# Mixture-of-experts stage: fewer buffers for the returning rows of the first image, and other places for their sums and transposes

## The chip, the cores and the metric

The kernel runs on one core of a Trainium2 chip. The metric is the device time of one execution in microseconds (us). The core's engines work side by side: TensorE (PE) multiplies matrices and transposes, VectorE (DVE) and ScalarE (ACT) work on elements, GpSimd (POOL) does so too and issues gathers, and SyncE (SP) issues plain transfers. Each engine takes its instructions in the order in which the program was laid out, so an instruction that waits holds up all that stand behind it on its engine. Transfers (DMAs) run on 16 DMA engines that all queues share.

## The reference

Four layers are applied in turn to x of shape (2, 128, 56, 56), each as x = x + layer(group_norm(x)): an attention, a 3x3 convolution, a mixture of experts on 2x2 patches, and a pair of Mamba scans. The change lies in the third layer, where its result is handed to the fourth:

```python
xp = patches(group_norm(x))                # 1568 tokens of 512 numbers, 784 of each image
probs = softmax(xp @ router_w)             # 8 experts
topv, topi = top_k(probs, 2); topv = topv / topv.sum()
for e in range(8):
    val, g = split(xp @ w1[e], 2)          # w1[e]: 512 x 2048
    out += gate[:, e:e+1] * ((val * sigmoid(g)) @ w2[e])    # w2[e]: 1024 x 512
x = x + unpatch(out)
```

The fourth layer begins with the group norm of this x, image by image.

## The kernel before, in words

**Routing.** Every token goes to two experts. The tokens are sorted by image and expert into tiles of 128 slots (`SLOTS`); `route` works out which expert serves each tile, which token fills each slot, and in which two slots each token's results will lie (`self.slots`). Two numbers are known when the program is laid out: the first 25 tiles (`fewest`) always exist, and the tiles 0 to 19 (`ahead` is 20) are sure to hold all that belongs to the first image. How many tiles there are beyond 25 is read at run time (`tc.Switch`); with these inputs there are 28.

**One tile** (`run`, lines 1323 to 1448). A gather of token rows (`xr`, an indirect DMA on POOL's queue, four buffers), four transposes on PE (`xr_ps`, L1369) and a copy on DVE (`xs_c`, L1371). Then `up`: 128 PE instructions with the first weight matrix (`h_ps`, L1380), in four parts of 32: for each half c of the hidden numbers first the gate's part and then the value's. ACT takes the sigmoid of the gate (`sg`, L1392), DVE multiplies (`ht`, L1394). Then `down`: 16 PE instructions with the second matrix (`o_ps`, L1400); ACT scales by the token's share (`ot`, L1403) and stores the tile to `os` in DRAM from its own queue (L1404). `down` of tile j-1 stands behind `up` of tile j.

**Weights.** SP loads the first matrix of a tile (4096 KB, L1341) and the second (2048 KB, L1347), each into one of two buffers. The second matrix's load waits for the `down` that used its buffer last, and the first matrix's load of the next tile stands behind it in SP's queue.

**The way back for the first image** (`combine`, lines 1450 to 1497, as a generator driven by `arrive`). The image has seven blocks of 112 tokens. For each block, `fetched` issues two gathers from `os` on POOL's queue (L1314, tiles `g0` and `g1`, 112 rows of 2 KB each), one for each of the token's two experts. DVE adds the two (L1486), PE transposes the sum in four pieces (`y_ps`, L1489), and one turn later DVE adds these to x (L1462) and takes the statistics (L88). After the last block come three turns for the group norm (L100, L104, L116). `LEAD` tells how many blocks are gathered before the first sum; `gathered` gives each table `LEAD + 1` buffers. A gather can reuse its buffers when the block that held them has been transposed.

**The order of the work.** One `next(beside)` is one turn of that generator. `turns` tells for each of the tiles 20 to 24 (keys 0 to 4) at which of five spots turns are taken: 0 to 3 are the ends of the four parts of `up`, 4 is the end of `down` of the tile before. In `spot`, `issue_after(traced[0])` places what the turn issues on PE behind the last PE instruction traced, and `issue_after(shaped[0])` does the same on DVE. POOL gets no such tie. Within these bounds a planner lays out each engine's order, by the program's order and by what it holds ready. What is left over of the generator runs before the Switch.

Of the kernel before, what the change touches and what calls it, by code (L numbers as in the profile page):

```python
# [1013 lines left out]
class PatchExperts:  # L1014
# [308 lines left out]
    def run(self, wpool, work, ps, beside):  # L1323
# [25 lines left out]

        traced, shaped = [None], [None]  # L1350

        turns = {0: (4, 4), 1: (1, 3), 2: (0, 1, 4), 3: (0, 1, 2, 3, 4), 4: (0, 0, 1, 2)}

        def spot(j, at):
            if j < self.fewest:
# [149 lines left out]

MAMBA_STATES, MAMBA_RANK, MAMBA_TAPS = 16, 8, 4

LEAD, LEAD2 = 5, 3

POOLED = {"f": (0, 1, 2, 8, 9), "b": (0, 1, 10, 11)}  # L1510

# [139 lines left out]
def mamba_pair(net, out, wts, combine, keep, norms):  # L1651
# [19 lines left out]
    with ExitStack() as ctx:  # L1671
# [425 lines left out]
        with tc.manual_schedule(engines={E.PE, E.Activation, E.DVE, E.Pool, E.SP}):  # L2097
            second = arrive_by_scalar(net, combine, 1, gathered, wide_bank, mm, keep, norms, LEAD2)
            first = min(agenda)
            for step in range(first, 0):  # L2100
                run(step)
                for _ in range((LEAD2, 0, 0, 0, 0, 0, 1, 0, 1, 0, 1, 1, 3, 1)[step - first] if step - first < 14 else 0):
                    next(second, None)
                fetch(step + 1)
        with tc.manual_schedule(engines={E.PE, E.Activation, E.DVE, E.Pool, E.SP}):
# [5 lines left out]
            for n, (h, u) in enumerate(units):  # L2111
                if n + 1 < len(units):
                    who, i = units[n + 1]
                    who.decay(i)
                fetch(n)
                if u % 2 == 0 and not (h.by_pool(u) and h.by_pool(u + 1)):
                    h.read_out(u)
                if u % 2 == 0 and n + 6 < len(units):
                    who, i = units[n + 6]
                    who.send_c(i // 2)  # L2120
                if n + 4 < len(units):
                    who, i = units[n + 4]
                    who.push(i)
                h.scan(u)
                if done:
                    done.pop().close()
                waiting.append((h, u))
                if n in (9, 13):
                    place["tag"] = "mm"
                    next(second)  # L2130

                quota = 0 if u == 3 and n > 3 else 2 if u == 7 and n > 7 else 1
                for _ in range(quota):
                    if len(waiting) > 3:
                        who, i = waiting.pop(0)
                        who.collect(i)
                        if i == UNITS - 1:
                            done.append(who)
                run(n)
# [4 lines left out]
            for step in range(len(units), max(agenda) + 1):  # L2144
                run(step)
                fetch(step + 1)
# [111 lines left out]
```

## Time and profile before

| what | value |
|---|---|
| median of 3 runs | 3005.71 us (3002.7 to 3007.07) |
| the profiled execution's own time | 3010.8 us |
| its span in the trace | 3009.1 us |
| PE busy | 2688.4 us (89% of the span) |
| DVE busy | 2180.9 us (72%) |
| ACT busy | 1854.5 us (62%) |
| POOL busy | 1446.6 us (48%) |
| DMA moved | 369.30 MB |
| tiles of experts on PE, first to last | about 1030 to 1656 us |
| gathers of the first image, first and last issue | 1493.0 and 1515.7 us |
| its transposes, first and last | 1514.8 and 1559.4 us |

The trace gives each instruction's start and duration from the span's start, and in brackets how long its engine was idle before it and whose end released it. A view of stretches gives, for each stretch of time, the busy time of each engine, the granted share of the TensorE clock (PEclk) and the share of time in which the DMA engines were busy. "DMA to landing" is the time from the issue of a transfer to the arrival of its last bytes.

### The profile page before, as it was taken

To read this page: it belongs to the slowest core of one execution; us is meant where nothing else is said; L and a number is where in the kernel's file an instruction comes from. 1 tells how busy PE (TensorE), PEld (TensorE's weight loads), DVE (VectorE), ACT (ScalarE), POOL (GpSimd) and SP (SyncE) were. 2 spreads that over 40 slices of the span, in tenths; PEclk is the share of its full clock that TensorE was granted. 3 is DMA by queue.
4 is the path that set the end of the run, shared out by engine and by line. 5 is a ranking of instruction groups with operands and counts; after the bars stand their busy time and mean duration, and the time that the engine had idled before them with its cause. 6 is when DMAs were issued, how large, how long until landed. Compare 5 with 4: busy or idle time off the path is not lost. (4 is left out here: it accounts for less than half of the span.)

```text
span 3009.1 us, 39362 instructions
## 1 busy us (share of the span) xinstructions
PE 2688.4 (89%) x14926; PEld 1273.6 (42%) x14926; DVE 2180.9 (72%) x1849; ACT 1854.5 (62%) x2951; POOL 1446.6 (48%) x792
## 2 busy tenths in 40 slices
PE   7999999999999799999999788888888888888874
PEld 3333333333325687878777323333333333233321
DVE  5978999999886400010020589999999999999996
ACT  5778778887761100000011588888888888988884
POOL 3000010001232100000110689999999999999995
PEclk9999999999989799999999889999999889999987
DMA  1000000000002587878885644555555465544460
GB/s 56 1 1 1 1 1 1 1 1 1 1 1 61 208 317 296 328 301 321 321 305 211 146 117 114 122 136 139 119 121 117 117 142 128 129 115 121 117 145 26
DMA packets 158222, 369.30 MB, mean 123 GB/s; under 512 B 25190, under 2 KB 115398, under 8 KB 154422
## 3 DMA queue, kind: packets, MB, share of 16 engines
q1 hardware_dynamic: 135778, 339.30, 37.6%
q0 software_dynamic: 5136, 14.70, 1.6%
q10 hardware_dynamic: 17092, 12.53, 1.3%
q8 instruction: 122, 2.00, 0.3%
q14 instruction: 94, 0.77, 0.1%
HBM read 297.89 MB, written 17.20 MB: 105 GB/s over the span
## 5 line engine op out<-in xcount | busy, mean ns | idle before, releaser
L1940 POOL TENSOR_TENSOR dBu<-dtu,Bs 128x896 f32<-128x896 f32 x448 | 922.0, 2093 | 22.3 <-DMA Cs<-far 6.6
L1959 DVE TENSOR_TENSOR_SCAN h<-dA,dBu 128x896 f32<-128x896 f32 x448 | 882.2, 2008 | 34.1 <-ACT dA L1929 29.5
L620 ACT ACTIVATE ex<-sc 128x896 f32<-128x896 f32 (+1 forms) x700 | 602.7, 917 | 129.2 <-PE sc L617 117.7
L1981 PE MATMUL y<-h,both 128*64 128x448 f32 x1792 | 464.1, 609 | 82.8 <-POOL h L1968 75.7
L627 DVE TENSOR_TENSOR ex_sum<-ex_sum,ex 128x1792 f32<-128x1792 f32 (+1 forms) x238 | 492.5, 2069 | 37.8 <-ACT ex L620 23.8
L1380 PEld LDWEIGHTS h_ps<-xs_c,w 128*128 128x128 f32 x3584 | 407.7, 194 | 27.3 <-ACT ot L1403 15.4
L1380 PE MATMUL h_ps<-xs_c,w 128*128 128x128 f32 x3584 | 412.5, 278 | 7.2 <-DMA w<-in_L_conv_w_dram 5.8
L617 PE MATMUL sc<-q,k 32*128 32x448 f32 (+1 forms) x2800 | 405.6, 590 | 3.3 <-ACT ex L620 2.7
L1970 DVE TENSOR_TENSOR h<-h,c_ps 128x1792 f32<-128x1792 f32 (+1 forms) x168 | 326.5, 1944 | 28.8 <-ACT c_ps L1947 11.3
L635 PE MATMUL av<-ex,va 128*32 128x448 f32 (+1 forms) x2800 | 337.0, 556 | 0.1
L1394 DVE TENSOR_TENSOR ht<-h_ps,sg 128x512 f32<-128x512 f32 x56 | 38.5, 691 | 395.7 <-PE h_ps L1380 338.8
L582 POOL TENSOR_TENSOR a_e<-a_e,a_inv 112x784 f32<-112x784 f32 x14 | 41.6, 2974 | 586.3 <-ACT ex L620 394.5
L1929 ACT ACTIVATE dA<-dt,f_A 128x448 f32<-128x448 f32 x448 | 282.7, 635 | 51.1 <-DVE h L1959 43.4
L1929 ACT ACTIVATE dA<-dt,b_A 128x448 f32<-128x448 f32 x448 | 282.9, 635 | 32.7 <-DVE h L1959 23.8
L1981 PEld LDWEIGHTS y<-h,both 128*64 128x64 f32 x1792 | 117.9, 146 | 352.5 <-issue 209.9
L1314 POOL DMA_INDIRECT xr<-xd,whom x28 | 28.1, 1004 | 487.0 <-PE xr_ps L1369 445.9
L1968 POOL TENSOR_TENSOR h<-h,Cs 128x1792 f32<-128x1792 f32 (+1 forms) x70 | 252.7, 3610 | 11.2 <-PE conv_ps L1802 4.3
L617 PEld LDWEIGHTS sc<-q,k 32*128 32x128 f32 (+1 forms) x2800 | 138.3, 182 | 232.0 <-issue 133.8
L1392 ACT ACTIVATE sg<-h_ps 128x512 f32<-128x512 f32 x56 | 33.4, 597 | 307.3 <-PE h_ps L1380 307.2
L1400 PE MATMUL o_ps<-w,ht 128*128 128x512 f32 x448 | 201.3, 593 | 1.2 <-DVE ht L1394 1.2
L1403 ACT ACTIVATE ot<-o_ps,share 128x512 f32<-128x512 f32 x28 | 19.2, 687 | 246.5 <-PE o_ps L1400 246.5
L625 DVE TENSOR_TENSOR ex_sum<-ex 128x1792 f32<-128x1792 f32 x56 | 114.4, 2042 | 56.4 <-ACT ex L620 56.4
(366 smaller groups left out, 2982.9 us busy)
## 6 DMA issues: line engine op xcount, KB each, us to landing
w<-in_L_conv_w_dram SPq DMA_DIRECT2D x28, 4096.0 KB, 20.2
w<-in_L_conv_w_dram SPq DMA_DIRECT2D x28, 2048.0 KB, 10.3
Cs<-far SPq DMA_DIRECT2D x448, 112.0 KB, 2.9
Bs<-far SPq DMA_DIRECT2D x54, 896.0 KB, 8.3
dtu<-sp_u SPq DMA_DIRECT2D x108, 224.0 KB, 3.8
dt<-dt SPq DMA_DIRECT2D x108, 224.0 KB, 4.9
os<-ot ACTq DMA_DIRECT2D x28, 256.0 KB, 7.9
xd<-xt SPq DMA_DIRECT2D x14, 224.0 KB, 2.7
```

The source lines that it names most:

```text
L617: nc.tensor.matmul(sc[:size, j, :BLK], self.m.k[rows, at : at + size], self.q[rows, :], start=True, stop=True)
L620: nc.scalar.activation(ex[:size, 2 * g : 2 * g + 2, :], sc[:size, :, :BLK], AF.Exp, scale=scale)
L627: nc.vector.tensor_add(self.total[g][:size], self.total[g][:size], ex[:size])
L635: nc.tensor.matmul(self.av[rows, :BLK], self.m.va[:size, i, rows], self.ex[i][:size, h, :], start=i == 0, stop=i == STEPS - 1,)
L1380: mm = nc.tensor.matmul(h_ps[:, i * SLOTS : (i + 1) * SLOTS], w1[:, q, f0 : f0 + P], xc[:, q, :], start=q == 0, stop=q == 3,)
L1400: mm = nc.tensor.matmul(o_ps, ht[:, i, :], w2[:, i, :], start=i == 0, stop=i == nj - 1)
L1929: nc.scalar.activation(self.dA[u][:, r * BLK : (r + 1) * BLK], self.dt2[:, m, r, :], AF.Exp, scale=self.w.A[:, j, 2 * m + r : 2 * m + r + 1],)
L1940: nc.gpsimd.tensor_tensor(self.dBu[u], self.dtu2[:, m], self.B[:, j, :].unsqueeze(1).to_broadcast(shape), ALU.mult)
L1959: nc.vector.tensor_tensor_scan(hf, af, bf, 0.0, ALU.mult, ALU.add)
L1968: nc.gpsimd.tensor_tensor(h4, h4, self.C[j].unsqueeze(1).to_broadcast(shape), ALU.mult)
L1970: nc.vector.tensor_tensor(h4, h4, self.c_ps[:, :BLK].unsqueeze(1).to_broadcast(shape), ALU.mult)
L1981: nc.tensor.matmul(self.y[r * H : (r + 1) * H, m, :BLK], both, self.hc[j][:, m, r, :], start=False, stop=j == PAIRS - 1)
```

## The change

`LEAD` falls from 5 to 1: one block instead of five is gathered ahead of the first sum, and each of the two tables has two buffers instead of six. The generator has twelve turns instead of sixteen, and `turns` places them anew:

```diff
-        turns = {0: (4, 4), 1: (1, 3), 2: (0, 1, 4), 3: (0, 1, 2, 3, 4), 4: (0, 0, 1, 2)}
+        turns = {0: (4,), 1: (3, 4), 2: (1, 3), 3: (0, 1, 3), 4: (0, 1, 2, 3)}
...
-LEAD, LEAD2 = 5, 3
+LEAD, LEAD2 = 1, 3
```

Turn by turn, with tile and spot:

| step | before | after |
|---|---|---|
| gather of block 0 | 20, 4 | 20, 4 |
| gather of block 1 | 20, 4 | 21, 3 |
| gathers of blocks 2 and 3 | 21, 1 and 21, 3 | 21, 4 and 22, 1 |
| gathers of blocks 4, 5, 6 | 22, 0; 22, 1; 22, 4 | 22, 3; 23, 0; 23, 1 |
| sum and transposes of block 0 | 22, 1 | 21, 3 |
| of block 1 | 22, 4 | 21, 4 |
| of blocks 2 and 3 | 23, 0 and 23, 1 | 22, 1 and 22, 3 |
| of blocks 4 and 5 | 23, 2 and 23, 3 | 23, 0 and 23, 1 |
| of block 6 | 23, 4 | 23, 3 |
| last addition to x | 24, 0 | 24, 0 |
| the norm's three turns | 24, 0; 24, 1; 24, 2 | 24, 1; 24, 2; 24, 3 |

The numbers of gathers, sums, transposes and additions stay as they were. `LEAD2`, for the second image, is unchanged.

## The prediction

> **What bounds the kernel here.** I first cut the end of the expert stage into tile cycles, each from one load of a second weight matrix to the next, in the view of stretches (columns: stretch, its length, busy us of PE, PEld, DVE, ACT and POOL, granted clock, DMA share, GB/s).
>
> ```profile
> 1462.03:1483.84 21.81, 21.81 (x150) 17.64 (x148) 2.08 (x4) 1.89 (x4) 1.00 (x2) 1.00 0.79 313
> 1483.84:1504.96 21.12, 21.12 (x146) 17.20 (x145) 1.84 (x3) 1.21 (x3) 8.83 (x9) 1.00 0.98 356
> 1504.96:1528.61 23.65, 22.32 (x154) 18.18 (x153) 4.71 (x10) 1.88 (x3) 7.27 (x7) 1.00 1.05 343
> 1528.61:1559.59 30.98, 26.56 (x170) 22.42 (x170) 11.83 (x33) 1.89 (x3) 1.02 (x1) 0.89 0.65 262
> 1559.59:1582.30 22.71, 22.68 (x156) 18.21 (x155) 4.97 (x18) 5.62 (x8) 0.00 (x0) 1.00 0.74 291
> ```
>
> The first row is a plain tile: PE never rests, and 21.81 us is its own work. DVE, ACT and POOL are nearly idle. So time is lost here only where PE waits, works slowly, or has more to do. The last four rows, with the returning image in them, take 98.46 us against 4 x 21.81 = 87.24: 11.2 too many. PE's timeline names them (start, us, instructions, idle time before).
>
> ```profile
> 1498.76 6.17 PE L1400 MATMUL o_ps<-w,ht 128*128 128x512 f32 x14
> 1504.77 0.60 PE L1369 MATMUL xr_ps<-ident,xr 128*128 128x128 f32 x4
> 1505.21 1.02 PE L1400 MATMUL o_ps<-w,ht 128*128 128x512 f32 x2
> 1507.56 7.38 PE L1380 MATMUL h_ps<-xs_c,w 128*128 128x128 f32 x64 [1.33 <-DMA w<-in_L_conv_w_dram]
> ...
> 1534.75 6.17 PE L1380 MATMUL h_ps<-xs_c,w 128*128 128x128 f32 x32 [4.42 <-DMA w<-in_L_conv_w_dram]
> ...
> 1541.22 3.75 PE L1380 MATMUL h_ps<-xs_c,w 128*128 128x128 f32 x32
> ```
>
> Tiles 22 and 23 wait 1.33 and 4.42 us for their first weight matrix. After the second wait 32 instructions take 6.17 us instead of 3.75: the clock is down, 2.42 us more. Seven blocks of four transposes delay their successors 0.45 us each, 3.2. Sum 11.4, so the excess is explained. Why the weights are late is in POOL's timeline and the landings.
>
> ```profile
> 1483.84 1.00 POOL L1314 DMA_INDIRECT xr<-xd,whom  x1 [20.81 <-PE xr_ps L1369]
> 1493.01 1.00 POOL L1314 DMA_INDIRECT g<-os,at_i  x1 [8.17 <-DMA w<-in_L_conv_w_dram]
> 1494.31 0.98 POOL L1314 DMA_INDIRECT g<-os,at_i  x1 [0.30 <-issue]
> ...
> 1515.68 0.98 POOL L1314 DMA_INDIRECT g<-os,at_i  x1 [0.74 <-PE y_ps L1489]
> ```
>
> Fourteen gathers leave in 23 us, 14 x 112 x 2 KB = 3.2 MB beside 6.3 MB of weights per tile. The first cannot leave sooner: it needs tile 19 in DRAM. (The releaser named is a weight load; the store of tile 19, issued at 1483.9 with stores landing in some 8 us, is the one that fits 1493.) Their landings, in the views of this source line for 1492 to 1503, 1505.8 to 1512, and the gather at 1515.7; then the first weight matrices in undisturbed cycles:
>
> ```profile
> DMA to landing us min/median/max: 12.3/12.4/13.8
> ...
> DMA to landing us min/median/max: 7.6/7.7/8.2
> ...
> DMA to landing us min/median/max: 15.0/15.0/15.0
> ...
> DMA to landing us min/median/max: 20.1/20.4/21.0
> ```
>
> What makes 12 to 15 out of 8 shows in the DMA view of 1497.5 to 1503 (queue, packets, MB, share): q1 carries the first weight matrix, q0 the gathers.
>
> ```profile
> q1 hardware_dynamic: 56, 1.74, 86.2%
> q0 software_dynamic: 65, 0.24, 12.0%
> ```
>
> Packet for packet they alternate, but a weight packet has 1.74 MB / 56 = 31 KB and a gather packet 3.7 KB. While a first weight matrix flows, a gather crawls.
>
> **What goes.** Spread over three tiles, the gathers no longer pile up in front of the weights, so both weight waits and the slow clock may go: 1.33 + 4.42 + 2.42 = 8.2 us, the most that can be won. Instruction counts are equal: 28 sums, transposes and gathers less or more: none.
>
> **What comes: block 0.** Its gathers keep their place (1493.01, 1494.31), since nothing ahead of them moved. The second landed 13.8 us later, at 1508.1; DVE's sum (0.69 us) followed at 1508.2. Fewer gathers behind it don't help: q0 serves them in order. Its transposes now stand behind `up` of tile 21, which ends at 1498.76 (there `down` of tile 20 begins). PE would wait from 1498.76 to 1508.9: **10.15 us**. Behind the waiting transposes on PE stand `down` of tile 20, the transposes of tile 22's tokens and its `up`; SP's next weight loads wait for that `down` too. Behind the waiting sum on DVE stand at most the product `ht` and copy `xs_c`, wanted later than the transposes. With a 7.7 us landing the wait would be 3.9.
>
> Two rules of the Trainium skill bear on this. "DMA: Bandwidth & Descriptors" (the SWDGE part of the anatomy of a DMA) fits a POOL-issued transfer by 2.0 us plus bytes over 436 GB/s, 2.5 us for 229 KB: block 0 would be there at 1496.8, no wait arise, and the sum be a gain of 8.2, 2997.5. The row says 12 to 15 beside weights, and I take the row. "TensorE: Matmul & The Clock Gate" (the HAM clock gate) says an idle window of about 3.4 us halves the clock until as long a busy one: 1.7 us lost by it, 2.42 by the row after 4.42 idle, none after 1.33. I take 2.4 for each wait above 3.4; by the rule the sum is 1.4 lower.
>
> **Then on the shifted clock.** Transposes 0 at 1508.9 (0.45), `down` 6.0 + 2.4 slow, transposes 1 at 1517.8 (its gathers landed by 1510), 1.46 for tokens and one product as at 1504.77: `up` of 22 begins at 1519.7, weights long there. Transposes 2 at 1526.9, 3 at 1534.6, `down` to 1541.0, `up` of 23 at 1542.5. Its weights, issued 1518.4, need 20.4 + 2.3 (two blocks' 0.92 MB at 0.4 MB/us): 1541.1, in time. A gather now waits for the transposes two blocks earlier: block 2's is released at 1509.4, 17 us ahead of use; block 3's 16; block 4's 19; block 5's 15 (with 1.3 between two issues and 14 to land, none to spare at worst).
>
> **Block 6.** Released by transposes 4 (end 1546.6), second issue 1547.9, while tile 24's first weight matrix (issued 1541.6, 20.4 long) flows: landing after 12.3 to 15.0, take 14, near the single late gather: 1561.9, sum to 1562.6. Its transposes stand behind `up` of 23, at 1557.8. PE waits **4.8 us** (3.1 to 5.8; none at 7.7), and 2.4 slow.
>
> The norm's last turn comes one spot later, behind `up` of tile 24: two 0.14 us matmuls as before; its ACT and DVE chain (some 4.5 us, then 0.77 for ACT's first `pad`) lies beside the 6.0 us `down` of tile 23. If that cover were gone, about 1 us. The token gathers of tiles 26 and 27 may stand behind later gathers on POOL; they have over 40 us. SP gets no other order. The freed buffers may move the scan stage's tiles: nothing, -1 to +1 as bounds.
>
> **Sum.** -8.2 + 10.15 + 2.4 + 4.8 + 2.4 = +11.6 us. The profiled execution took 3010.8 (span 3009.1 and 1.7 around it), 5.1 above the median of runs; the difference is carried to the median: 3005.7 + 11.6 = **3017.3 us**. Its own range, from the bounds of both waits and clock: 3012 to 3023.
>
> **Rivals.** *The planner puts the sum of block 0 later*: it did slip one product of the next `down` in while `xs_c` was copied (1505.21), so it fills gaps it foresees. But all seven transposes stood at their turns. If `down` of tile 20 goes first, the wait shrinks to 1508.9 - 1504.8 = 4.1: -8.2 + 4.1 + 0 to 2.4 (clock) + 0 to 7.2 (block 6) = -4.1 to +5.5, say 3006.5. *Block 6 is hidden anyway* (lands in 8 or its place slips): -8.2 + 12.55 = +4.4, 3010. *Faster*: the gathers land early enough that no transposes wait, since only four are out at a time: 3005.7 - 8.2 = 2997.5. It decides when block 0's second gather lands by 1498.1, 3.8 us after issue; and a gain over 0.2% remains while new waits are under 2.2 us. Against it speaks 13.8. *More waits*: block 5 or the weights of 23 come late as well, +4 to +7 with clock: 3023.
>
> **How the numbers follow.** Likeliest case 0.50; more waits 0.07; later place 0.18; block 6 hidden 0.12; faster 0.13. The bound of what can be told from no change is 0.2%, 6 us. Slower: 0.50 + 0.07 + 0.04 of the later place + 0.03 of block 6 hidden = 0.64; same 0.23; faster 0.13. The range 3001 to 3023 takes in the middle cases and leaves out the full gain (about 0.12) and the worst waits (about 0.05).
>
> **What would show it.** Right: transposes 0 on PE at about 1508.9 with 10 us idle before and `down` of tile 20 behind them; half clock after; no weight wait at tiles 22 and 23; about 5 us idle before transposes 6; the norm some 12 us later. Wrong: `down` of 20 still at 1498.8, a landing of block 0 well before 1507, or weight waits that remain.

## The result, and the profile after

The changed kernel takes 3015.38 us (median of 6 runs, 3013.31 to 3017.39) against 3004.44 for the kernel before (6 runs, 3001.77 to 3007.07): a ratio of 1.0036, 95% interval 1.0025 to 1.0046. That is 10.9 us slower; 11.6 was forecast. Its profiled execution took 3014.52 us with a span of 3012.7.

Up to the place of the change this execution is 4.6 us ahead of the one shown of before (tile 25's token gather starts at 1479.26 instead of 1483.84), so its clock times are compared after adding 4.6. PE's timeline of the changed kernel, with the same columns as before:

```profile
1503.66 1.02 PE L1489 MATMUL y_ps<-ident,g 112*128 112x112 f32 x4 [9.32 <-DVE g L1486]
1504.48 7.57 PE L1400 MATMUL o_ps<-w,ht 128*128 128x512 f32 x14
...
1513.77 7.38 PE L1380 MATMUL h_ps<-xs_c,w 128*128 128x128 f32 x64
...
1537.92 3.81 PE L1380 MATMUL h_ps<-xs_c,w 128*128 128x128 f32 x32 [1.36 <-DMA w<-in_L_conv_w_dram]
...
1557.73 0.70 PE L1489 MATMUL y_ps<-ident,g 112*128 112x112 f32 x4 [4.33 <-DVE g L1486]
1558.27 7.88 PE L1400 MATMUL o_ps<-w,ht 128*128 128x512 f32 x14
```

The first line is block 0: PE waits 9.32 us for DVE's sum, and the fourteen instructions of `down` behind it take 7.57 us instead of 6.17, since the clock is down. The weights of tile 22 are there without a wait; those of tile 23 still cost 1.36. The last two lines are block 6: 4.33 us of waiting, and again a slow `down`.

POOL's timeline shows when the gathers leave and what releases them:

```profile
1488.43 1.00 POOL L1314 DMA_INDIRECT g<-os,at_i  x1 [8.17 <-DMA w<-in_L_conv_w_dram]
1489.73 0.98 POOL L1314 DMA_INDIRECT g<-os,at_i  x1 [0.30 <-issue]
...
1503.88 0.98 POOL L1314 DMA_INDIRECT g<-os,at_i  x1 [10.60 <-DVE g L1486]
...
1537.30 0.98 POOL L1314 DMA_INDIRECT g<-os,at_i  x1 [0.31 <-DVE g L1486]
1542.47 0.98 POOL L1314 DMA_INDIRECT g<-os,at_i  x1 [4.19 <-PE y_ps L1489]
```

The last two are block 6's. The second table's buffer is free as soon as DVE has summed block 4, the first table's only when PE has transposed it; so only the last gather is late. The landings of this line's gathers, for the four that leave from 1488, the three from 1503.8, and the last:

```profile
DMA to landing us min/median/max: 11.6/12.7/14.0
...
DMA to landing us min/median/max: 3.3/3.4/3.4
...
DMA to landing us min/median/max: 14.3/14.3/14.3
```

The middle line is new. The `down` that PE's wait holds up ends only at 1512, SP's next load stands behind it (issued 1512.08), and so the gathers have the DMA engines to themselves: from 1503.5 to 1512 the DMA view names one queue alone (queue, packets, MB, share).

```profile
q0 software_dynamic: 241, 0.69, 28.7%
```

The same tile cycles as shown of before, in the view of stretches:

```profile
1457.45:1479.26 21.81, 21.81 (x150) 17.64 (x148) 2.08 (x4) 1.89 (x4) 1.00 (x2) 1.00 0.81 313
1479.26:1512.08 32.82, 23.50 (x150) 18.61 (x149) 4.40 (x10) 1.21 (x3) 7.86 (x8) 0.84 0.72 257
1512.08:1535.30 23.22, 23.22 (x162) 19.06 (x162) 6.04 (x15) 1.89 (x3) 5.99 (x6) 1.00 0.95 335
1535.30:1566.19 30.89, 25.21 (x162) 19.72 (x161) 8.02 (x21) 1.88 (x3) 2.97 (x3) 0.94 0.68 244
1566.19:1588.44 22.25, 22.25 (x154) 18.09 (x153) 5.07 (x18) 5.62 (x8) 0.00 (x0) 1.00 0.78 298
```

The plain tile is the same 21.81 us. The four cycles behind it, counted from SP's load of a second matrix at 1478.58 to the one at 1588.44, take 109.9 us; in the trace of before they took 99.1 (1483.16 to 1582.30). The difference is 10.7 us, the whole loss: what follows takes no longer than before (1424.3 us against 1426.8), so it does not lie in the scan stage behind.

### The profile page after: what moved, and what is told of

Same layout as the page of the kernel before. It is cut to its first block, busy times and chain, and to the rows that moved or that the text cites. A ratio compares the mean times of both kernels' runs of the same rounds, so it can differ in the third digit from the quotient of the medians.

```text
span 3012.7 us, 39367 instructions
## 1 busy us (share of the span) xinstructions
PE 2682.6 (89%) x14926; PEld 1271.2 (42%) x14926; DVE 2180.9 (72%) x1849; ACT 1855.1 (62%) x2951; POOL 1446.9 (48%) x792
## 5 line engine op out<-in xcount | busy, mean ns | idle before, releaser
L1970 DVE TENSOR_TENSOR h<-h,c_ps 128x1792 f32<-128x1792 f32 (+1 forms) x168 | 326.5, 1944 | 28.8 <-ACT c_ps L1947 11.2
```

The source lines that it names most:

```text
L1970: nc.vector.tensor_tensor(h4, h4, self.c_ps[:, :BLK].unsqueeze(1).to_broadcast(shape), ALU.mult)
```

## The experiments

Each kernel below was timed beside the kernel before, whose median in these comparisons lay between 3003.2 and 3005.8 us. "The four cycles" are those just described, in the profiled execution: 99.1 us before, 109.9 changed.

**Two buffers, block 0 one turn later.** If the place of block 0's sum is what costs, moving it behind `down` of tile 20 should help.

```diff
-        turns = {0: (4,), 1: (3, 4), 2: (1, 3), 3: (0, 1, 3), 4: (0, 1, 2, 3)}
+        turns = {0: (4,), 1: (4, 4), 2: (1, 3), 3: (0, 1, 3), 4: (0, 1, 2, 3)}
```

> The changed kernel with one turn moved: block 0 is summed and transposed behind the second product of tile 20 (spot 4 of tile 21, together with block 1), two buffers as changed. Theory of two late gathers: the 9.3 us wait of TensorE for block 0 shrinks by the 6.0 us of that product to about 3.5, its slow clock goes or stays small (0 to 1.8), the 1.36 us weight wait at tile 23 goes, the 4.3 us wait for block 6 stays. About 7 to 9 us less than the changed kernel: 3006 to 3008 against its 3015.4. Rival, that the cost is that of fewer buffers wherever the sums lie: within 2 us of 3015. Rival, that the cost lies in the scan stage behind it: 3015.

Measured: 3020.61 us, ratio to the kernel before 1.0053 (1.0039 to 1.0066); four cycles 113.1 us. By the four cycles it is 3.2 us slower than the changed kernel (the intervals of the two ratios overlap), which none of the theories expected. PE's timeline of this kernel:

```profile
1502.66 1.02 PE L1489 MATMUL y_ps<-ident,g 112*128 112x112 f32 x4 [3.40 <-DVE g L1486]
...
1523.04 0.99 PE L1489 MATMUL y_ps<-ident,g 112*128 112x112 f32 x4 [6.33 <-DVE g L1486]
...
1559.28 1.00 PE L1489 MATMUL y_ps<-ident,g 112*128 112x112 f32 x4 [4.39 <-DVE g L1486]
```

The wait for block 0 did shrink to 3.40, the weight wait went, and block 6 kept its 4.39. But the slow clock did not go: over the 6.5 us behind the first wait the granted clock is 0.51, a loss of some 3 us, where 0 to 1.8 was expected. And block 2 now costs 6.33. Because `down` of tile 20 was no longer held up, SP loaded the next weights at 1499 instead of 1512, and the gathers issued from 1504.2 to 1506.8 met them. In this kernel they landed after

```profile
DMA to landing us min/median/max: 12.9/16.3/16.6
```

where those released behind the long wait of the changed kernel took 3.4. The long wait had paid for the next gathers; with it gone, the wait moved on. In each of the three kernels with two buffers and unsplit weight loads (the changed one, this one, and the one with the old places below) some block came late.

**Six buffers, new places.**

```diff
-        turns = {0: (4,), 1: (3, 4), 2: (1, 3), 3: (0, 1, 3), 4: (0, 1, 2, 3)}
+        turns = {0: (4, 4, 4, 4, 4), 1: (3, 4), 2: (1, 3), 3: (0, 1, 3), 4: (0, 1, 2, 3)}
...
-LEAD, LEAD2 = 1, 3
+LEAD, LEAD2 = 5, 3
```

> The changed places of the sums, but five blocks gathered ahead and six buffers a table as before. Theory of two late gathers: the wait for block 0 stays at 9 to 10 us with 1.8 of slow clock, because its gathers leave and land as before; the wait for block 6 goes, because its gathers leave 25 us earlier; the weights of tile 23 come in time since TensorE is late anyway. About 6 to 8 us less than the changed kernel: 3007 to 3009, still 3 to 5 above the kernel before. Rival, that two buffers alone make the loss: 3004. Rival, that the places alone make it: 3015.

Measured: 3011.62 us, ratio 1.0020 (1.0012 to 1.0029); four cycles 102.6. The only wait left is block 0's:

```profile
1504.87 1.02 PE L1489 MATMUL y_ps<-ident,g 112*128 112x112 f32 x4 [9.97 <-DVE g L1486]
```

So the places alone lose time, by block 0, and the two buffers lose more, by block 6. By the four cycles the loss over the kernel before is 3.4 us, as expected (3 to 5); in the runs it is 6, and what makes the difference stays open.

**Two buffers, old places.**

```diff
-        turns = {0: (4,), 1: (3, 4), 2: (1, 3), 3: (0, 1, 3), 4: (0, 1, 2, 3)}
+        turns = {0: (4,), 1: (), 2: (1, 4), 3: (0, 1, 2, 3, 4), 4: (0, 0, 1, 2)}
```

> The places of the sums as before, but one block gathered ahead and two buffers a table as changed. Theory: blocks 0 and 1 cause no wait; the sums of blocks 3 to 6 stand 4 to 10 us apart on TensorE while each gather is released only two blocks earlier and lands 8 to 15 us later, so TensorE waits two or three times there, 8 to 14 us in all with 2 to 4 of slow clock; the weight wait at tile 23 falls from 4.4 to under 1.5 and its slow clock goes. Together 3 to 11 us more than the kernel before: 3007 to 3015. Rival, that the places alone make the loss: 3004 or, with the weight wait gone, 2998.

Measured: 3013.53 us, ratio 1.0035 (1.0022 to 1.0048); four cycles 107.3. The size was right, the form was not: not several waits, but one of 12.49 us at block 4; nothing at tile 23's weights, 0.87 at tile 22's.

```profile
1550.14 0.99 PE L1489 MATMUL y_ps<-ident,g 112*128 112x112 f32 x4 [12.49 <-DVE g L1486]
```

The gather that block 4's sum waited for left at 1534.83, landed 14.4 us later, and met a first weight matrix on its way. By the order of the releases it could have left at 1529.6, when the transposes of block 2 had freed its buffer. But on POOL it stood behind a gather that waited until 1533.5 for the sum of block 3.

**Four buffers, old places.** One step between: enough buffers that no sum waits, fewer gathers at once.

```diff
-        turns = {0: (4, 4), 1: (1, 3), 2: (0, 1, 4), 3: (0, 1, 2, 3, 4), 4: (0, 0, 1, 2)}
+        turns = {0: (4, 4), 1: (3,), 2: (1, 4), 3: (0, 1, 2, 3, 4), 4: (0, 0, 1, 2)}
...
-LEAD, LEAD2 = 5, 3
+LEAD, LEAD2 = 3, 3
```

> The places of the sums as before, three blocks gathered ahead and four buffers a table. Theory: four blocks' gathers leave at once as before, those of blocks 4, 5 and 6 only behind the transposes of blocks 0, 1 and 2, each 15 us or more ahead of their use, so no sum waits; 0.9 MB less competes with the first weight matrix of tile 23, so its wait falls from 4.4 to about 2 us and the clock stays up: 2 to 5 us less than the kernel before, 2999 to 3002. Rival, that the first eight gathers make that wait: 3004 as before. Rival, that block 5 or 6 comes late: 3006 or more.

Measured: 3000.06 us, ratio 0.9991 (0.9972 to 1.0010); four cycles 93.3. One of its 14 executions took 3037.6 us, and the interval includes no change; so it was measured once more:

> The run with four buffers and the old places once more, to narrow its interval beside the kernel before: theory, 4 to 6 us less than the kernel before (ratio 0.998 to 0.999); rival, that the first measurement was chance: within 2 us of it.

Measured: 2999.44 us, ratio 0.9979 (0.9971 to 0.9987); four cycles 93.2. It beats both kernels: by the medians 6 us less than before and 16 less than the changed one. In this second execution no sum waits, and what is left of the weight waits is

```profile
1501.16 7.38 PE L1380 MATMUL h_ps<-xs_c,w 128*128 128x128 f32 x64 [0.77 <-DMA w<-in_L_conv_w_dram]
...
1525.28 3.81 PE L1380 MATMUL h_ps<-xs_c,w 128*128 128x128 f32 x32 [1.35 <-DMA w<-in_L_conv_w_dram]
```

against 1.33 and 4.42 before; the 32 instructions behind the second take 3.81 us, not 6.17: after a wait of 1.35 the clock stays up.

**Four buffers, block 0 alone at the changed place.**

```diff
-        turns = {0: (4, 4), 1: (3,), 2: (1, 4), 3: (0, 1, 2, 3, 4), 4: (0, 0, 1, 2)}
+        turns = {0: (4, 4), 1: (3, 3), 2: (4,), 3: (0, 1, 2, 3, 4), 4: (0, 0, 1, 2)}
```

> As the run with four buffers and the old places, but with the sum and transposes of block 0 alone at the changed kernel's place, behind the up products of tile 21. Theory: this one place costs TensorE a wait of 9 to 10 us and 1.8 of slow clock, and hides the two weight waits of 1.0 and 1.2 us: 8 to 10 us more than the run with the old places (3000.1), 3008 to 3010. Rival, that the wait is made up by loads that come in meanwhile: within 2 us of 3000.

Measured: 3008.74 us, ratio to before 1.0016 (1.0008 to 1.0024), 9 us more than with the old place by the medians (8 to 11 by the ratios, as one or the other of its two measurements is taken); four cycles 102.1 against 93.2. PE's wait for block 0 is 9.18 us and there is no weight wait:

```profile
1503.01 1.02 PE L1489 MATMUL y_ps<-ident,g 112*128 112x112 f32 x4 [9.18 <-DVE g L1486]
```

With 1.87 us of slow clock behind it this place costs 11.05, where the prediction had 10.15 + 2.4; it hides the weight waits of 0.77 and 1.35, which leaves 8.9.

**The changed kernel, weights in smaller packets.** This tests why a gather is late. Only tiles 22 to 24 are touched.

```diff
-            dma = nc.sync.dma_start(w1, w1s[e].rearrange("o c q f -> (o c) q f"))
+            given = w1s[e].rearrange("o c q f -> (o c) q f")
+            if 22 <= j <= 24:
+                for q in range(4):
+                    dma = nc.sync.dma_start(w1[:, q, :], given[:, q, :])
+            else:
+                dma = nc.sync.dma_start(w1, given)
```

> The changed kernel, with the first weight matrices of tiles 22, 23 and 24 each loaded by four transfers of 1 MB whose packets are 8 KB instead of 32. Theory that a gather crawls because it takes turns with large packets: block 0's gathers, issued as before, land after 9 to 11 us instead of 13 to 14, so the wait for block 0 shrinks from 9.3 to 5 to 7 us; block 6's late gather lands after 9 to 11 instead of 14.3 and its wait of 4.3 with its slow clock goes; the weights themselves land about a microsecond later. Together 6 to 10 us less than the changed kernel: 3006 to 3010. Rival, that a gather is late because of the bytes in flight whatever their packets: landings of 13 to 14, 3015 as the changed kernel.

Measured: 3005.45 us, ratio 1.0010 (1.0002 to 1.0018); four cycles 100.2. The DMA view from 4.9 us after the first gather's issue, for 5.5 us (1492.5 to 1498):

```profile
q1 hardware_dynamic: 165, 1.20, 72.8%
q0 software_dynamic: 167, 0.49, 29.4%
```

The weights' packets are 7.3 KB now (1.20 MB / 165) instead of 31. As in the stretch shown of before, about as many packets of the one queue pass as of the other; so twice as much of the gathers does, 0.49 MB in 5.5 us instead of 0.24 (0.22 in the changed kernel, 1492.9 to 1498.4). The landings of block 0's and 1's gathers, and of block 6's last one:

```profile
DMA to landing us min/median/max: 9.5/10.9/12.2
...
DMA to landing us min/median/max: 8.2/8.2/8.2
```

instead of 11.6/12.7/14.0 and 14.3. Block 0's wait fell from 9.32 to 5.56 us, block 6's from 4.33 to none, the weight wait of tile 23 from 1.36 to 1.04. The bytes are the same and only the transfers are split, so the bytes alone do not make a gather this late. The packet counts point at the size of the weights' packets; the number of transfers changed with it, and no run separates the two.

The packets' size is not the whole delay either. The DMA view, read in steps of half a microsecond, has the first packets of block 0's first gather 4.0 to 4.5 us after its issue in this kernel and in the changed one alike. For a gather alone (issued 1503.88 in the changed kernel) they come after 1.5 to 2.0 us. The smaller packets shorten what follows the first packet.

**The kernel before, with the same split.**

> The kernel before, with the same split of the weight loads of tiles 22, 23 and 24. Theory: no sum waits there, so earlier gathers win nothing; the gathers now take their share ahead of the weights, whose waits stay (4.4 at tile 23) or grow by up to 2 us (1.3 at tile 22): 3004 to 3008. Rival, that the split itself costs or wins time beyond the gathers: below 3002 or above 3009.

Measured: 3003.47 us, ratio 1.0001 (0.9993 to 1.0010). The wait at tile 23 (4.42), which was to stay, is gone, and the one at tile 22 has grown from 1.33 to 3.71, with a slow clock behind it (0.79 over 8.2 us). That fits gathers that take more of the engines and so make weights late; where no sum waits for gathers, the runs show nothing won. In the profile the four cycles take 96.6 us, 2.5 less than before; this gain does not show in the runs, and why stays open. With the loads split in both kernels, the change costs about 2 us (3005.45 against 3003.47; the intervals of the two ratios overlap) instead of 11.

**Three buffers, blocks 4 to 6 one place later.**

```diff
-        turns = {0: (4, 4), 1: (3,), 2: (1, 4), 3: (0, 1, 2, 3, 4), 4: (0, 0, 1, 2)}
+        turns = {0: (4, 4), 1: (), 2: (1, 4), 3: (0, 1, 3, 4), 4: (0, 1, 1, 2, 3)}
...
-LEAD, LEAD2 = 3, 3
+LEAD, LEAD2 = 2, 3
```

> Two blocks gathered ahead, three buffers a table, and the sums of blocks 4, 5 and 6 one place later than before (block 6 inside the up products of tile 24). Theory: with six gathers instead of eight at the start and the late ones with 15 us or more until their use, no sum waits and the weight waits of tiles 22 and 23 (1.0 and 1.2 with four buffers) fall to about 0.5 each: 1 to 2 us less than with four buffers, 2998 to 3000. Rival, that block 5 or 6 comes late with three buffers: one wait of 2 to 5 us, 3002 to 3006.

Measured: 2999.80 us, ratio 0.9983 (0.9977 to 0.9990); four cycles 93.5: as good as four buffers, not better. Tile 23's weights come in time, but tile 22's still cost 0.90 us and tile 24's now 1.58. The gathers' bytes have to pass somewhere, and here part of them pass one tile later.

## Why the prediction was right

The forecast was 3017.3 us and the direction slower; measured are 3015.4 and slower. The two waits that it named came, at the blocks that it named and from late gathers. By its steps:

**What goes, -8.2.** The wait at tile 22 went. The one at tile 23 fell from 4.42 to 1.36 and took the slow clock with it. So 6.8 went. The step that failed is "Its weights ... 1541.1, in time": SP's load of them (issued 1512.64) landed 25.1 us after its issue, not 22.7. The delay over the 20.4 of an undisturbed cycle was 4.7 us and not 2.3. I had counted two blocks' gathers; in POOL's timeline five gathers of two and a half blocks and one token gather leave early enough to cross these weights. At the prediction's 0.4 MB/us their 1.4 MB make an estimated 3.5 us; the rest stays open.

One reading of before was off as well: the prediction began its four cycles at POOL's token gather (1483.84) and not at SP's load (1483.16). From load to load the four take 99.1 us, 11.9 more than four plain tiles and not 11.2; its terms explain 11.4 of that.

**Block 0, 10.15 + 2.4.** The planner put the transposes exactly where the prediction had them, the gathers left where they had left before, and PE waited 9.32 us, since block 0's second gather landed 13.1 us after its issue instead of 13.8. The run with block 0 alone at this place shows the wait by itself (9.18, and 9 us in the time). There eight gathers leave in a row and here four, and the second lands after 13.1 us in both: fewer gathers behind it did not help, as the prediction said. (In the kernel before, too, seven gathers from block 0's second on landed in the order of their issue, from 1508.1 to 1514.3.)

**Block 6, 4.8 + 2.4.** PE waited 4.33, its last gather landing 14.3 us after issue (14 was taken). What the prediction had wrong is the release: not both gathers behind the transposes, but the second table's behind the sum, so it left 5 us ahead of the other. The late one was issued 0.9 us sooner than assumed and took 0.3 longer.

**Slow clock.** The term was too large: `down` and the transposes lost 1.77 us behind block 0 (7.57 - 6.17 and 0.82 - 0.45) and 1.78 behind block 6 (7.88 - 6.19 and 0.54 - 0.45). I had taken 2.42 from the one row of before and set aside the estimate of 1.7 that the HAM clock gate section of the Trainium skill's page "TensorE: Matmul & The Clock Gate" leads to; here that was nearer. For the gathers it was the other way round: the estimate of 2.5 us by the fit in "DMA: Bandwidth & Descriptors" (anatomy of one DMA, SWDGE path) would have made the change a gain, and 11.6 to 14.3 were measured beside first weight matrices. Alone, a gather took 3.3 to 3.4, nearer the fit.

**Sum.** -6.8 + 9.3 + 1.8 + 4.3 + 1.8 = +10.4, where the four cycles show +10.7 and the runs +10.9. The prediction's +11.6 has the gain too large by 1.4 and the losses too large by 2.6. That the sum came within a microsecond is in part luck, since these errors cancel; the direction is not, as the two waits alone (13.6) outweigh the most that could be won (8.2).

**The rivals.** That the planner would put block 0 later did not happen; the run that forced it shows that it would have been worse (3020.6) and not better (3006.5), because SP's next loads then start earlier and meet the gathers that follow (6.33 us at block 2), which that rival had not counted. That the gathers would land early, with four of them out, did not happen (11.6 to 14.0). That fewer gathers at a time win is true by itself, as the run with four buffers shows; it is what the change's other half gives away.

## What to carry to other kernels

A transfer's time depends on its company: look up how long it takes beside the transfers that will be in flight at its new place, and count from what releases it, per buffer. A buffer fewer turns a gather from "early" into "released by the step before last", and where the latency is longer than the steps between, the engine waits. Removing one such wait can move the next gather into other traffic, so recompute the chain and don't subtract. Between too many gathers at once (weights late, six buffers) and too few (sums late, two buffers) the best of those tried lay: four buffers at the old places, or three with later ones.

## What the runs showed of the hardware

- The same gather of 112 rows of 2 KB lands after 3.3 to 3.4 us alone (changed kernel, from 1503.9), about 7 to 9 beside a weight matrix in 2 KB packets (7.7 and 7.8 in the changed kernel, where 430 packets carry 0.88 MB from 1513.5 to 1517), and 11.6 to 16.8 where a first weight matrix in 31 KB packets is in its way. With that matrix in 7.3 KB packets it was 8.2 to 12.9. That it is so quick alone, and that it can take two to five times as long by what it meets, I had not expected in this size.
- No more than eight of POOL's gathers were out at once. With six buffers and the new places the ninth left at 1502.29, after a wait for the first, which landed at 1501.5, and the tenth at 1504.30, after the second at 1504.0; their buffers were free. So more than four buffers a table could not send more ahead at first.
- PE's wait can empty the DMA engines, because SP's next load waits for the `down` that PE holds up: behind the 9.3 us wait three gathers landed in 3.4 us each, and without it the ones in their place took up to 16.6.
- PE's waits of 0.8 to 1.6 us left the clock up in every run here; those of 3.4 to 12.5 us lowered it. The cost was 1.5 to 2.4 us in most places and did not grow with the wait: the largest, some 3 us, stood behind the shortest (3.40, in the run with block 0 one turn later, where a further 0.43 us followed).
